# Values of two successive key tiles in one group of matmuls in the first attention, with a planner that prices changes of form on TensorE

## The chip, the cores and the metric

The kernel runs on one core of a Trainium2 chip. The metric is the device time of one execution in microseconds (us). Eight images pass through four layers in one launch. The core's engines are called PE (TensorE matmuls; PEld is its weight load), DVE (VectorE), ACT (ScalarE), POOL (GpSimd) and SP (SyncE, which here issues transfers).

## The reference, cut to what matters

An input `x` of 8 images with 256 channels and 32x32 pixels goes through four residual layers, each after a group norm. The first is an attention of 8 heads over the 1024 pixels, the second and third are 3x3 convolutions, the fourth is a mixer (four selective scans, gates, depthwise convolutions, a second attention, norms). The change touches the first layer:

```python
def _L0_conv_ref(x, w_qkv, w_out, b_out):
    HEADS, DIM_HEAD, SCALE, EPS = 8, 64, 10.0, 1e-12
    b, c, hh, ww = x.shape
    n = hh * ww
    qkv = jnp.einsum('bcxy,oc->boxy', x, w_qkv)
    q, k, v = jnp.split(qkv, 3, axis=1)
    q, k, v = (t.reshape(b, HEADS, DIM_HEAD, n) for t in (q, k, v))
    q, k = _l2norm_last(q), _l2norm_last(k)
    sim = jnp.einsum('bhdi,bhdj->bhij', q, k) * SCALE
    attn = jax.nn.softmax(sim, axis=-1)
    out = jnp.einsum('bhij,bhdj->bhid', attn, v)
    ...
    return jnp.einsum('bcxy,oc->boxy', out, w_out) + b_out[None, :, None, None]

x = x + _L0_conv_ref(_gn(x), ...)   # first attention
x = x + _L1_conv_ref(_gn(x), ...)   # 3x3 convolution
x = x + _L2_conv_ref(_gn(x), ...)   # 3x3 convolution
x = x + _L3_conv_ref(_gn(x), ...)   # mixer: scans, second attention, norms
return x
```

## The kernel before

**Streams and the planner.** The kernel's code does not issue its instructions in the order in which it is written. Every engine call is recorded (`Recorded`, line 252 makes the call later, so all planned work carries that line in the profile), with the stream it belongs to: A is the first attention (`front_attention`), O its output projection, C the two convolutions, N, F0 to F3, S and Z0 to Z3 the scans of the mixer, B and E its rest. Each stream exists once for each image. `Plan.issue` hands the records to `arrange`, which chooses one order for every engine. The streams of several images are mixed: while image 5 is in its first attention, image 4 is in its scans and image 3 in its second attention.

**How the order is made.** `gather` joins recorded matmuls into groups that are placed as a whole. `appraise` gives each group a length (`holds`). For matmuls it adds one length for each pass and a surcharge from the table `STAGGER`, by the form of the array: 64x128 means that the stationary operand has 64 rows and 128 columns. `rank` gives each group a due time, interpolated from the table `PACE`, which holds 4 marks for each stream and image. `arrange` plays the program forward with these lengths: on every engine it takes, of the groups that can start earliest, the one of the first rank (`pick`). When the next group on PE has another form than the last, 100 ns are added. The result is a fixed program order on each engine; on the chip each engine runs its own order and waits on semaphores.

**The first attention.** Heads go in pairs (`pair`): four pairs for an image, and for each pair two halves of 512 queries (`h`) and eight tiles of 128 keys (`kt`), so 64 units for an image. `scores` writes a unit's scores for both heads into one PSUM tile of 128x1024 (`big`, a pool of two buffers that almost all other matmuls share), by two matmuls of the form 64x128 that lie beside each other on different rows of the array; ACT then makes `p`, the exponential, in one instruction. `values` multiplies `p` with V into one PSUM tile `acc` (one buffer), by two matmuls of the form 128x64 that lie beside each other on different columns; eight units accumulate in one `acc`. DVE adds the `p` of an odd unit to that of the even one before it, and for every half four such sums go through `ones` (128x32 matmuls, `big<-p,ones`) to give the softmax's denominators. `p` tiles come from a pool of 12 buffers that most streams share. In the recorded order, `values` of a unit stands two units behind its `scores`: scores 2, values 0, scores 3, values 1, and so on.

In the profile one matmul of the program shows as two records, so a pair of scores is `big<-q,k` x4 and a pair of values is `acc<-p,v` x4. The second attention also writes `acc<-p,v` (and `cv<-p,v`); its code is not touched.

Of the kernel before, what the change touches and what calls it, by code (L numbers as in the profile page):

```python
# [25 lines left out]
NKT = N // P  # L26
# [5 lines left out]
ENGINES = {"PE": 0, "DVE": 1, "Activation": 2, "Pool": 3, "SP": 4}  # L32
TABLES = {"Exp": 1, "Abs": 1, "Tanh": 5, "Ln": 2, "Gelu": 4}
WINDOW = 3413.33
STAGGER = {(128, 128): 5, (64, 128): 109, (128, 64): 56, (128, 32): 29, (32, 128): 90}
CLAIMED = (("vp", "v"), ("xp", "x"))
OUT_OF_TURN = {("ps_big", "big")}
PACE = {
    "A": (
        (-682, -424, -117, -25),  # L40
        (516, 618, 694, 732),
        (1009, 1111, 1211, 1320),
        (1607, 1675, 1748, 1823),
        (2135, 2205, 2285, 2342),
        (2665, 2733, 2806, 2909),
        (3195, 3278, 3368, 3454),
        (3714, 3781, 3854, 3902),
    ),
    "B": (
        (1368, 1444, 1509, 1584),  # L50
        (1923, 1981, 2040, 2094),
        (2413, 2483, 2561, 2631),
        (2909, 2939, 3105, 3156),
        (3483, 3566, 3655, 3734),
        (4003, 4099, 4197, 4313),
        (4492, 4492, 4513, 4700),
        (5658, 5715, 5736, 5740),
    ),
    "C": (
        (268, 286, 475, 478),  # L60
        (226, 890, 1004, 1104),
        (1251, 1399, 1527, 1655),
        (1776, 1933, 2060, 2185),
        (2284, 2453, 2596, 2729),
        (2985, 3045, 3116, 3245),
        (3380, 3514, 3656, 3802),
        (3926, 4001, 4174, 4291),
    ),
    "E": (
        (1584, 1624, 1671, 1704),  # L70
        (2139, 2161, 2194, 2229),
        (2639, 2685, 2724, 2761),
        (3178, 3208, 3256, 3277),
        (3704, 3752, 3787, 3816),
        (3976, 3978, 4015, 4017),
        (4691, 4842, 5048, 5087),
        (4451, 4453, 4775, 4871),
    ),
    "F0": (
        (435, 494, 498, 499),  # L80
        (863, 968, 998, 1025),
        (499, 905, 905, 905),
        (608, 740, 740, 987),
        (1145, 1145, 1194, 1203),
        (1745, 1746, 1865, 1865),
        (3530, 3530, 3570, 3570),
        (2244, 2362, 2402, 2421),
    ),
    "F1": (
        (488, 661, 706, 713),  # L90
        (1324, 1375, 1376, 1386),
        (1814, 1825, 1853, 1909),
        (2387, 2404, 2435, 2467),
        (2826, 2842, 2888, 2939),
        (3472, 3479, 3485, 3495),
        (3877, 3894, 3932, 3935),
        (4379, 4441, 4506, 4578),
    ),
    "F2": (
        (760, 818, 839, 866),  # L100
        (1108, 1355, 1361, 1397),
        (1896, 1929, 1932, 2020),
        (2337, 2337, 2456, 2476),
        (2961, 2989, 2989, 3066),
        (3215, 3469, 3469, 3572),
        (3973, 4011, 4055, 4097),
        (4582, 4590, 4590, 4590),
    ),
    "F3": (
        (976, 979, 984, 1044),  # L110
        (1537, 1537, 1540, 1610),
        (2056, 2068, 2077, 2097),
        (2557, 2557, 2558, 2621),
        (3063, 3088, 3122, 3170),
        (3673, 3679, 3738, 3747),
        (4139, 4163, 4163, 4176),
        (4723, 4723, 4723, 4723),
    ),
    "N": (
        (-178, -178, -178, -178),  # L120
        (830, 830, 858, 860),
        (986, 986, 986, 998),
        (1734, 1734, 1734, 1734),
        (2043, 2043, 2043, 2043),
        (2294, 2297, 2315, 2323),
        (3328, 3374, 3374, 3374),
        (3310, 3532, 3543, 3563),
    ),
    "O": (
        (551, 553, 553, 558),  # L130
        (711, 711, 758, 828),
        (1298, 1319, 1360, 1374),
        (1850, 1851, 1863, 1863),
        (2373, 2401, 2418, 2418),
        (2891, 2915, 2915, 2915),
        (3458, 3480, 3482, 3486),
        (3923, 3923, 3928, 3928),
    ),
    "S": (
        (700, 900, 1070, 1202),  # L140
        (1245, 1449, 1589, 1768),
        (1761, 1972, 2117, 2288),
        (2279, 2491, 2632, 2808),
        (2832, 3034, 3177, 3349),
        (3344, 3565, 3701, 3868),
        (3878, 4092, 4264, 4402),
        (4841, 4852, 4853, 4853),
    ),
    "V": (
        (-584, -584, -364, -358),  # L150
    ),
    "Z0": (
        (796, 817, 859, 884),
        (1326, 1328, 1334, 1394),
        (1870, 1875, 1911, 1983),
        (2394, 2406, 2565, 2581),
        (2926, 2932, 2948, 2948),
        (3101, 3128, 3148, 3389),
        (3955, 3972, 3994, 4136),
        (4523, 4524, 4533, 4664),  # L160
    ),
    "Z1": (
        (687, 722, 730, 1159),
        (1431, 1453, 1457, 1554),
        (1971, 1990, 1992, 2018),
        (2454, 2496, 2509, 2607),
        (3049, 3055, 3071, 3091),
        (3562, 3574, 3585, 3627),
        (4091, 4091, 4099, 4159),
        (4701, 4701, 4701, 4719),  # L170
    ),
    "Z2": (
        (1011, 1011, 1011, 1011),
        (1595, 1595, 1659, 1674),
        (2072, 2072, 2075, 2076),
        (2615, 2622, 2635, 2656),
        (3215, 3216, 3218, 3222),
        (3561, 3561, 3561, 3568),
        (4204, 4250, 4250, 4250),
        (4758, 4759, 4759, 4759),  # L180
    ),
    "Z3": (
        (1299, 1312, 1326, 1326),
        (1709, 1734, 1745, 1865),
        (2260, 2284, 2383, 2388),
        (2794, 2795, 2812, 2836),
        (3329, 3334, 3339, 3339),
        (3847, 3848, 3855, 3867),
        (4301, 4301, 4341, 4393),
        (4764, 4836, 4836, 5061),  # L190
    ),
    "H": (
        (-2577, -2577, -2577, -2577),
        (-1990, -1988, -1950, -1759),
        (-2961, -2961, -2961, -2312),
        (-2311, -2311, -2311, -2311),
        (-1439, -1439, -1439, -1439),
        (-1171, -1171, -1171, -1168),
        (-608, -608, -608, -608),
        (-633, -633, -633, -411),  # L200
    ),
}

# [189 lines left out]
def gather(ops):  # L393
    groups, of = [], []
    for n, op in enumerate(ops):
        last = groups[-1] if groups else None
        if op["engine"] == 0:
            out, lhs = op["outs"][0], op["ins"][0]
            (rows, at), (width, to) = place(lhs), place(out)
            op["array"], op["at"] = (rows, width), (at, to)  # L400
            if last and (last.array, last.stream) == (op["array"], op["stream"]):
                first = ops[last.ops[0]]["outs"][0]
                if elements(out) <= P:
                    joins = len(last.ops) < 16
                elif op["array"] != (P, P):
                    joins = len(last.ops) < 4 and all(
                        ops[k]["at"] != op["at"] for k in last.ops
                    )
                else:
                    joins = len(last.ops) < 3  # L410
                beside = first.tensor.name == out.tensor.name or rows == 32
                if joins and beside:
                    last.ops.append(n)
                    of.append(len(groups) - 1)
                    continue
        groups.append(Group(op, n))
        groups[-1].array = op.get("array")
        of.append(len(groups) - 1)
    return groups, of
# [39 lines left out]
def appraise(ops, groups, rooms):  # L459
    for g in groups:  # L460
# [18 lines left out]
        for op in (ops[n] for n in g.ops):  # L479
            n = elements(op["outs"][0])  # L480
            if op["array"] != (P, P) and n > P and beside and op["at"] not in beside:
                beside.add(op["at"])
                continue
            beside = {op["at"]}
            g.holds += max(n / 0.6, 215 if g.holds else 135) + STAGGER[op["array"]]
        g.takes = g.holds + 165


# [33 lines left out]
def arrange(ops, rooms):  # L522
# [110 lines left out]
    def pick(e):  # L633
        chosen, at = None, 0
        candidates = ready[e]
        while at < len(candidates):
# [10 lines left out]
            late = start  # L647
            if groups[n].table and not groups[n].table & table:
                late += 1200.0
            if (  # L650
                chosen is None
                or late < chosen[0] - 1e-9
# [34 lines left out]
    while len(order) < len(groups):  # L687
# [8 lines left out]
        if e == 0:  # L696
            if g.array != array:
                if array:
                    holds, takes = holds + 100.0, takes + 100.0
                array = g.array  # L700
            now, rest = start, holds
            pass_windows(now)
# [46 lines left out]
def preact_stack(ctx: ExitStack, tc: tile.TileContext, I, out, cols):  # L749
# [460 lines left out]
    def attention(pairs):  # L1210
# [24 lines left out]
            scalar.activation(p, s, AF.Exp)  # L1235
            u["p"] = p

        def values(u):
            pair, h, kt = pair_of(u["t"]), u["h"], u["kt"]
            if kt == 0:  # L1240
                pair["acc"] = acc_tile()
            for e in range(2):
                tensor.matmul(
                    pair["acc"][e * 64 : e * 64 + 64],
                    pair["v"][e](kt),
                    u["p"][:, HALVES[e]],
                    start=kt == 0,
                    stop=kt == NKT - 1,
                )
            if kt == 0:  # L1250
                pair["sums"] = []
            if kt % 2 == 0:
                pair["sums"].append(u["p"])
            else:
                total = pair["sums"][-1]
                vector.tensor_add(total, total, u["p"])
            if kt == NKT - 1:
                pair["take"](h, pair["acc"], pair["sums"])

        units = [  # L1260
# [2 lines left out]
            for h in range(2)  # L1263
            for kt in range(NKT)
        ]
        for n in range(len(units) + 2):
            if n + 8 < len(units):
                pair_of(units[n + 8]["t"])
            for stage, at in ((scores, n), (values, n - 2)):
                if 0 <= at < len(units):  # L1270
                    stage(units[at])

    def front_attention(src, img, exact=False):
        img["src"] = src
# [1103 lines left out]
```

## Time and profile before

| | |
|---|---|
| median of 3 runs | 5156.42 us (5152.59 to 5157.5) |
| the profiled execution | 5152.86 us |
| its span, from first to last instruction | 5151.1 us |
| mean granted TensorE clock | 0.951 |
| matmuls of the program on PE | 9589 (19178 records) |

Engine lines give busy time, share of the span and number of instructions. A matmul's end in the profile is modelled, so successive matmuls overlap in the list by up to 0.2 us, and the distance from one start to the next is the safer number. In the list of engine groups the columns are operation, output and input tiles, form and shape, count, then busy us and mean ns of one, then the idle time before them with who ended it.

| group | count | busy us | mean ns | idle before us |
|---|---|---|---|---|
| PE `acc<-p,v` 128*64, both attentions | 3072 | 837.1 | 625 | 39.3 |
| PE `cv<-taps,w` 128*128 | 3072 | 748.9 | 395 | 33.9 |
| PE `big<-q,k` 64*128, first attention | 2048 | 584.0 | 650 | 31.1 |
| PE `y<-hs,sel` 128*32, scans | 2048 | 312.7 | 627 | 62.7 |
| PE `big<-qk,qk` 32*128, second attention | 2048 | 302.9 | 649 | 5.1 |
| ACT `p<-big` | 1024 | 1014.6 | 1020 | 567.7 |

The first attention's matmuls of the eight images start at 51, 268, 776, 1385, 1996, 2586, 3205 and 3781 us; the last of them starts at 4024 us. The last scan's `y<-hs,sel` stands at 4852 us.

### The profile page before, as it was taken

How to read it: one execution, taken by the hardware profiler on the slowest of the kernel's cores; microseconds unless marked ns; L12 is line 12 of the kernel's file. 1: busy time of each engine (PE TensorE's matmuls, PEld its weight loads, DVE VectorE, ACT ScalarE, POOL GpSimd, SP SyncE). 2: the span in 40 equal slices, each digit the busy share in tenths (PEclk: the TensorE clock that was granted, in tenths of full speed). 3: DMA queues.
4: the chain of work that ended last, by engine and by line, in shares of the span. 5: the costliest groups of instructions: out<-in, count | busy, mean ns of one | idle time of the engine just before them, and what ended most of it. 6: DMA issues, size and time to landing. Idle time of an engine off the chain costs nothing.

```text
span 5151.1 us, 53923 instructions
## 1 busy us (share of the span) xinstructions
PE 4757.1 (92%) x19178; PEld 1946.1 (38%) x19178; DVE 4037.5 (78%) x5586; ACT 2911.2 (57%) x3829; POOL 17.8 (0%) x26
## 2 busy tenths in 40 slices
PE   8999899999999999999999999999999899898796
PEld 3262263253432534344442344325343343432323
DVE  3336989987988968889886988878878899799802
ACT  4426446656665565656656555655656457476352
POOL 0000000000000000000000000000000000000000
PEclk9999899999999999999999999999999999898897
DMA  4143354343333433334423343324333444334200
GB/s 137 39 126 99 107 163 130 96 151 114 117 113 96 137 107 112 112 115 127 131 93 101 115 152 114 122 70 151 122 98 112 126 137 152 94 126 130 78 19 25
DMA packets 256662, 575.20 MB, mean 112 GB/s; under 512 B 51192, under 2 KB 79224, under 8 KB 256384
## 3 DMA queue, kind: packets, MB, share of 16 engines
q1 hardware_dynamic: 167680, 431.11, 26.7%
q10 hardware_dynamic: 88704, 140.55, 8.9%
q8 instruction: 154, 2.52, 0.2%
q14 instruction: 124, 1.02, 0.1%
HBM read 483.18 MB, written 63.18 MB: 106 GB/s over the span
## 4 chain that ended last, share of the span: by engine, by line
PE 66%; DVE 20%; ACT 6%; DMA 4%; issue 3%; SPq 1%; ACTq 0%; DVEq 0%
PE big L252 38%; PE cv L252 14%; PE acc L252 12%; DVE hs L252 11%; PE y L252 3%; ACT p L252 2%; DVE room L252 1%; DVE xt L252 1%; DVE p L252 1%; DVE u L252 1%; DMA rs<-inv 1%; SPq L252 1%; DVE st L252 1%; ACT taps L252 1%; DMA du<-du_m 1%
## 5 line engine op out<-in xcount | busy, mean ns | idle before, releaser
L252 ACT ACTIVATE p<-big 128x1024 f32<-128x1024 f32 x1024 | 1014.6, 1020 | 567.7 <-PE big L252 508.1
L252 ACT ACTIVATE da<-dt,a_neg 128x512 f32<-128x512 f32 x1024 | 728.0, 720 | 554.5 <-DVE hs L252 435.0
L252 PE MATMUL acc<-p,v 128*64 128x512 f32 x3072 | 837.1, 625 | 39.3 <-ACT p L252 36.1
L252 PE MATMUL cv<-taps,w 128*128 128x256 f32 x3072 | 748.9, 395 | 33.9 <-DVE taps L252 17.1
L252 PEld LDWEIGHTS cv<-taps,w 128*128 128x128 f32 x3072 | 583.8, 195 | 285.9 <-issue 152.8
L252 DVE TENSOR_TENSOR hs<-du,bc 128x1024 f32<-128x1024 f32 x512 | 613.4, 1209 | 78.6 <-PE y L252 56.5
L252 DVE TENSOR_TENSOR hs<-hs,bc 128x1024 f32<-128x1024 f32 x512 | 621.5, 1214 | 32.4 <-ACT carry L252 30.8
L252 DVE TENSOR_TENSOR_SCAN hs<-da,carry,hs 128x512 f32<-128x512 f32 x512 | 636.9, 1268 | 3.0 <-ACT da L252 2.3
L252 PE MATMUL big<-q,k 64*128 64x512 f32 x2048 | 584.0, 650 | 31.1 <-ACT p L252 20.7
L252 DVE TENSOR_TENSOR_SCAN hs<-da,hs 128x512 f32<-128x512 f32 x512 | 607.8, 1210 | 4.2 <-ACT da L252 2.9
L252 DVE TENSOR_TENSOR p<-p 128x1024 f32<-128x1024 f32 x256 | 311.6, 1217 | 207.0 <-ACT p L252 129.1
L252 PEld LDWEIGHTS acc<-p,v 128*64 128x64 f32 x3072 | 162.1, 136 | 599.6 <-issue 414.2
L252 PE MATMUL y<-hs,sel 128*32 128x512 f32 x2048 | 312.7, 627 | 62.7 <-DVE hs L252 52.0
L252 PEld LDWEIGHTS big<-q,k 64*128 64x128 f32 x2048 | 160.0, 188 | 424.9 <-issue 198.1
L252 PE MATMUL big<-qk,qk 32*128 32x512 f32 x2048 | 302.9, 649 | 5.1 <-DVE z L252 2.8
L252 PE MATMUL cv<-p,v 128*64 128x512 f32 x1024 | 278.7, 612 | 0.0
L252 PE MATMUL big<-xn,w 128*128 128x512 f32 x512 | 232.1, 599 | 2.3 <-ACT big L252 1.1
L252 PE MATMUL big<-o,w 128*128 128x512 f32 x384 | 179.4, 610 | 5.8 <-DVE o L252 4.0
L252 PE MATMUL big<-room,w 128*128 128x512 f32 (+3 forms) x308 | 145.0, 625 | 29.1 <-ACT room L252 28.5
L252 PEld LDWEIGHTS big<-qk,qk 32*128 32x128 f32 x2048 | 84.3, 185 | 188.5 <-issue 144.8
L252 PEld LDWEIGHTS y<-hs,sel 128*32 128x32 f32 x2048 | 47.4, 109 | 268.0 <-issue 116.5
L252 DVE RECIPROCAL few_inv<-few 128x16 f32<-128x16 f32 (+1 forms) x48 | 13.4, 279 | 168.7 <-DMA few<-sums 168.2
(235 smaller groups left out, 5190.8 us busy)
## 6 DMA issues: line engine op xcount, KB each, us to landing
bc<-bc SPq DMA_DIRECT2D x256, 512.0 KB
w<-wc ACTq DMA_DIRECT2D x384, 256.0 KB
dt<-dt_m SPq DMA_DIRECT2D x128, 512.0 KB
du<-du_m SPq DMA_DIRECT2D x128, 512.0 KB
rs<-inv SPq DMA_DIRECT2D x64, 256.0 KB
raw<-xm SPq DMA_DIRECT2D x64, 256.0 KB
dt_m<-dt SPq DMA_DIRECT2D x128, 128.0 KB
du_m<-a SPq DMA_DIRECT2D x128, 128.0 KB
```

The source lines that it names most:

```text
L252: made = op["call"](*args, **kwargs).ins
```

## The change

Three things are edited, and all marks of `PACE` but none of its streams are new.

First, `values` takes two units and issues their four matmuls one after the other, and the loop records two scores, then the values of the two units before them. `gather` lets such a group hold each place of the array twice where the form is 64 columns wide. Second, the lengths: every pass gets 5 ns instead of the surcharge of `STAGGER`, and a change of form gets the time of the new form from `SWITCH` instead of 100 ns. Third, `pick` can add `STAY` to a group that would change the form; `STAY` is 0.

```diff
-STAGGER = {(128, 128): 5, (64, 128): 109, (128, 64): 56, (128, 32): 29, (32, 128): 90}
+SWITCH = {(128, 128): 203, (64, 128): 203, (128, 64): 152, (128, 32): 125, (32, 128): 205}
+STAY = 0
...
 PACE = {
     "A": (
-        (-682, -424, -117, -25),
-        (516, 618, 694, 732),
+        (-1119, -855, -558, -455),
+        (331, 431, 506, 507),
...
@@ gather
-                    joins = len(last.ops) < 4 and all(
-                        ops[k]["at"] != op["at"] for k in last.ops
-                    )
+                    again = sum(ops[k]["at"] == op["at"] for k in last.ops)
+                    joins = len(last.ops) < 4 and again < (2 if width == 64 else 1)
@@ appraise
-            g.holds += max(n / 0.6, 215 if g.holds else 135) + STAGGER[op["array"]]
+            g.holds += max(n / 0.6, 215 if g.holds else 135) + 5
@@ arrange, pick
+            if e == 0 and groups[n].array != array:
+                late += STAY
@@ arrange
                 if array:
-                    holds, takes = holds + 100.0, takes + 100.0
+                    opens = SWITCH[g.array]
+                    holds, takes = holds + opens, takes + opens
@@ attention
-        def values(u):
-            pair, h, kt = pair_of(u["t"]), u["h"], u["kt"]
-            if kt == 0:
-                pair["acc"] = acc_tile()
-            for e in range(2):
-                tensor.matmul(
-                    pair["acc"][e * 64 : e * 64 + 64],
-                    pair["v"][e](kt),
-                    u["p"][:, HALVES[e]],
-                    start=kt == 0,
-                    stop=kt == NKT - 1,
-                )
-            if kt == 0:
-                pair["sums"] = []
-            if kt % 2 == 0:
-                pair["sums"].append(u["p"])
-            else:
-                total = pair["sums"][-1]
-                vector.tensor_add(total, total, u["p"])
-            if kt == NKT - 1:
+        def values(two):
+            pair, h = pair_of(two[0]["t"]), two[0]["h"]
+            if two[0]["kt"] == 0:
+                pair["acc"], pair["sums"] = acc_tile(), []
+            for u in two:
+                for e in range(2):
+                    tensor.matmul(
+                        pair["acc"][e * 64 : e * 64 + 64],
+                        pair["v"][e](u["kt"]),
+                        u["p"][:, HALVES[e]],
+                        start=u["kt"] == 0,
+                        stop=u["kt"] == NKT - 1,
+                    )
+            total = two[0]["p"]
+            vector.tensor_add(total, total, two[1]["p"])
+            pair["sums"].append(total)
+            if two[1]["kt"] == NKT - 1:
                 pair["take"](h, pair["acc"], pair["sums"])
...
-        for n in range(len(units) + 2):
+        for n in range(0, len(units) + 2, 2):
             if n + 8 < len(units):
                 pair_of(units[n + 8]["t"])
-            for stage, at in ((scores, n), (values, n - 2)):
-                if 0 <= at < len(units):
-                    stage(units[at])
+            for u in units[n : n + 2]:
+                scores(u)
+            if n:
+                values(units[n - 2 : n])
```

More of the change, by code (lines that the diff above doesn't have):

```diff
@@ L39 @@
     "A": (
-        (-682, -424, -117, -25),
-        (516, 618, 694, 732),
[L42 to L47, printed above, removed]
+        (-1119, -855, -558, -455),
+        (331, 431, 506, 507),
+        (813, 915, 1000, 1064),
+        (1478, 1523, 1564, 1564),
+        (1948, 2014, 2097, 2098),
+        (2474, 2542, 2615, 2660),
+        (2997, 3097, 3118, 3190),
@@ L48 @@
+        (3549, 3613, 3672, 3680),
     ),
     "B": (
[L50 to L57, printed above, removed]
+        (1198, 1212, 1244, 1268),
+        (1724, 1773, 1840, 1882),
+        (2238, 2297, 2383, 2456),
+        (2724, 2743, 2917, 2973),
+        (3293, 3372, 3469, 3551),
@@ L58 @@
+        (3722, 3869, 3989, 4125),
+        (4252, 4255, 4256, 4293),
+        (5965, 6024, 6103, 6134),
     ),
     "C": (
[L60 to L67, printed above, removed]
+        (102, 103, 107, 176),
+        (8, 727, 835, 931),
+        (1109, 1262, 1389, 1512),
+        (1565, 1748, 1880, 2001),
@@ L68 @@
+        (2108, 2265, 2413, 2543),
+        (2776, 2824, 2889, 2994),
+        (3092, 3318, 3467, 3609),
+        (3846, 3846, 4009, 4121),
     ),
     "E": (
[L70 to L77, printed above, removed]
+        (1379, 1426, 1482, 1526),
+        (1894, 2004, 2040, 2098),
@@ L78 @@
+        (2447, 2490, 2536, 2558),
+        (2942, 2955, 3033, 3062),
+        (3516, 3564, 3602, 3629),
+        (3084, 3127, 3153, 3169),
+        (4319, 4566, 4664, 4933),
+        (3410, 3723, 4016, 4016),
     ),
     "F0": (
[L80 to L87, printed above, removed]
+        (-528, -454, -454, -307),
@@ L88 @@
+        (94, 189, 191, 320),
+        (-38, 112, 136, 170),
+        (-1532, -914, -900, -654),
+        (1191, 1358, 1378, 1378),
+        (-221, -163, -140, -140),
+        (858, 858, 858, 858),
+        (-629, -585, -583, 154),
     ),
     "F1": (
[L90 to L97, printed above, removed]
+        (353, 479, 485, 485),
@@ L98 @@
+        (1137, 1198, 1198, 1198),
+        (1608, 1613, 1662, 1717),
+        (2174, 2242, 2254, 2286),
+        (2688, 2717, 2749, 2788),
+        (3264, 3264, 3280, 3282),
+        (3725, 3729, 3741, 3741),
+        (4213, 4213, 4303, 4303),
     ),
     "F2": (
[L100 to L106, printed above, removed]
@@ L107 @@
-        (4582, 4590, 4590, 4590),
+        (560, 695, 695, 813),
+        (519, 962, 1006, 1042),
+        (1757, 1777, 1777, 1811),
+        (1940, 1940, 2253, 2302),
+        (2737, 2803, 2815, 2933),
+        (2996, 3110, 3258, 3310),
+        (3772, 3838, 3889, 3921),
+        (4219, 4332, 4335, 4338),
     ),
     "F3": (
[L110 to L114, printed above, removed]
@@ L115 @@
-        (3673, 3679, 3738, 3747),
-        (4139, 4163, 4163, 4176),
-        (4723, 4723, 4723, 4723),
+        (842, 856, 856, 858),
+        (1272, 1290, 1470, 1470),
+        (1866, 1885, 1999, 1999),
+        (2385, 2391, 2467, 2520),
+        (2843, 2899, 2917, 2955),
+        (3511, 3517, 3595, 3605),
+        (3965, 4032, 4041, 4064),
+        (4382, 4437, 4447, 4447),
     ),
     "N": (
[L120 to L127, printed above, removed]
+        (-1228, -1054, -931, -931),
+        (-368, -105, -103, 105),
+        (-355, -355, -355, -355),
+        (446, 821, 836, 840),
+        (529, 687, 687, 1658),
+        (1233, 1236, 1770, 1810),
+        (3189, 3608, 3608, 3608),
+        (2401, 2763, 2870, 3562),
     ),
     "O": (
-        (551, 553, 553, 558),
-        (711, 711, 758, 828),
-        (1298, 1319, 1360, 1374),
@@ L133 @@
[L133 to L137, printed above, removed]
+        (368, 368, 368, 368),
+        (566, 575, 600, 662),
+        (1118, 1122, 1154, 1180),
+        (1620, 1674, 1674, 1686),
+        (2183, 2215, 2231, 2233),
+        (2672, 2702, 2702, 2727),
+        (3263, 3286, 3289, 3290),
+        (3690, 3741, 3743, 3756),
     ),
     "S": (
-        (700, 900, 1070, 1202),
@@ L141 @@
[L141 to L147, printed above, removed]
+        (611, 740, 906, 1038),
+        (1061, 1267, 1436, 1583),
+        (1571, 1788, 1915, 2101),
+        (2086, 2301, 2440, 2616),
+        (2684, 2786, 2960, 3119),
+        (3176, 3369, 3537, 3705),
+        (3712, 3946, 4107, 4251),
+        (4585, 4585, 4586, 4591),
@@ L148 @@
     ),
     "V": (
-        (-584, -584, -364, -358),
+        (-2785, -2717, -2717, -2690),
     ),
     "Z0": (
[L153 to L160, printed above, removed]
+        (623, 671, 803, 811),
+        (1160, 1165, 1189, 1209),
+        (1628, 1675, 1795, 2335),
+        (2111, 2112, 2216, 2576),
@@ L161 @@
+        (2772, 2786, 2787, 2813),
+        (2956, 2956, 3025, 3280),
+        (3815, 3849, 3849, 4264),
+        (4259, 4323, 4386, 4445),
     ),
     "Z1": (
[L163 to L170, printed above, removed]
+        (571, 574, 574, 884),
+        (1203, 1271, 1274, 1292),
@@ L171 @@
+        (1710, 1710, 1710, 1718),
+        (2277, 2305, 2315, 2322),
+        (2851, 2854, 2854, 2903),
+        (3421, 3422, 3422, 3489),
+        (3937, 3942, 4015, 4158),
+        (4373, 4373, 4397, 4397),
     ),
     "Z2": (
[L173 to L180, printed above, removed]
+        (766, 872, 872, 1035),
@@ L181 @@
+        (1443, 1478, 1484, 1484),
+        (1820, 1851, 1886, 1914),
+        (2414, 2416, 2418, 2418),
+        (2889, 2895, 2933, 3034),
+        (3296, 3349, 3392, 3396),
+        (4051, 4088, 4158, 4158),
+        (4406, 4532, 4586, 4678),
     ),
     "Z3": (
[L183 to L189, printed above, removed]
@@ L190 @@
-        (4764, 4836, 4836, 5061),
+        (1050, 1056, 1131, 1136),
+        (1538, 1542, 1590, 1653),
+        (2072, 2072, 2206, 2214),
+        (2604, 2606, 2636, 2676),
+        (3159, 3163, 3166, 3175),
+        (3671, 3672, 3688, 3688),
+        (4180, 4184, 4195, 4245),
+        (4447, 4457, 4458, 4556),
     ),
     "H": (
[L193 to L197, printed above, removed]
@@ L198 @@
-        (-1171, -1171, -1171, -1168),
-        (-608, -608, -608, -608),
-        (-633, -633, -633, -411),
+        (-4008, -3991, -3987, -3915),
+        (-3151, -3119, -3088, -1884),
+        (-4487, -4154, -3535, -1882),
+        (-4782, -4677, -4620, -1309),
+        (-2758, -2480, -2285, -949),
+        (-2380, -2380, -2262, -995),
+        (-2906, -2264, -1774, 141),
+        (-997, -844, -684, 319),
     ),
```

## The prediction

> **What bounds the kernel now.** I read the engines' shares first, then the chain of work that ended last, then PE's list in order of time, then who waits for whom, and last the busy time by stages.
>
> ```profile
> PE 4757.1 (92%) x19178; PEld 1946.1 (38%) x19178; DVE 4037.5 (78%) x5586; ACT 2911.2 (57%) x3829; POOL 17.8 (0%) x26
> ```
>
> ```profile
> PE 66%; DVE 20%; ACT 6%; DMA 4%; issue 3%; SPq 1%; ACTq 0%; DVEq 0%
> ```
>
> PE is busy for 92% of the span and holds 66% of the chain; DVE holds 20% of the chain. So time taken from PE shortens the run in most places, and not where a scan on DVE ends last. PE's idle time is 5151.1 - 4757.1 = 394 us.
>
> The list of PE in order of time (start, length, line, operation, tiles, form, count, idle before):
>
> ```profile
> 405.69 1.08 PE L252 MATMUL acc<-p,v 128*64 128x512 f32 x4
> 406.70 1.13 PE L252 MATMUL big<-q,k 64*128 64x512 f32 x4
> ...
> 409.74 2.79 PE L252 MATMUL acc<-p,v 128*64 128x512 f32 x12
> 412.47 1.99 PE L252 MATMUL big<-q,k 64*128 64x512 f32 x8
> 414.72 1.13 PE L252 MATMUL big<-q,k 64*128 64x512 f32 x4 [0.27 <-ACT p L252]
> ```
>
> ```profile
> 909.31 1.13 PE L252 MATMUL big<-q,k 64*128 64x512 f32 x4
> 910.37 1.08 PE L252 MATMUL acc<-p,v 128*64 128x512 f32 x4
> 911.37 1.07 PE L252 MATMUL y<-hs,sel 128*32 128x512 f32 x8
> 912.37 1.13 PE L252 MATMUL big<-q,k 64*128 64x512 f32 x4
> ```
>
> The reader is to see the price of a change of form, from start to next start. A pair of values between other forms takes 406.70 - 405.69 = 1.01 us. Three pairs in one run take 412.47 - 409.74 = 2.73 us. Two pairs more cost 1.72 us, so a pair inside a run costs 0.86 us, and opening the run costs 1.01 - 0.86 = 0.15 us. In the same way a pair of scores costs 910.37 - 909.31 = 1.06 us, so its form opens for 0.20 us; the four `y` (0.86 us of passes) take 1.00 us, so 128x32 opens for 0.14 us. The `big<-u,mdtw` x4 of form 128x128, from 903.25 to 905.17 us, takes 1.92 us against four passes of 0.43 us, which is 0.20 us for opening. The last line of the first block shows what stands against the change: a third score in a row waited for ACT to empty one of the two `big` buffers.
>
> ```profile
> PE big L252 <- ACT p L252: 51.1, 38, 8.0
> PE acc L252 <- ACT p L252: 36.1, 55, 6.8
> ```
>
> These are PE's waits for the exponential (us in total, times, longest): 87.2 us in 93 waits.
>
> ```profile
> 3000.00:3500.00 500.00, 474.93 (x1974) 199.03 (x1973) 410.29 (x595) 289.29 (x376) 1.80 (x1) 0.98 0.37 114
> 4700.00:4800.00 100.00, 70.43 (x260) 24.80 (x252) 98.44 (x104) 58.82 (x84) 1.80 (x1) 0.79 0.36 110
> ```
>
> The stages (window, length, busy us of PE, PEld, DVE, ACT, POOL, PE's granted clock, DMA share, GB/s) show PE as the bound while the first attentions run, up to 4024 us, and DVE as the bound in the last image's scan at 4700 us.
>
> **The change part by part.** *The work itself.* Both programs hold 9589 matmuls, and equal numbers of exponentials, DVE additions and DMAs (616 on ACT's queue, 1731 on SP's). One load of an activation table goes, 79 to 78, 1283 ns on ACT, which is 57% busy; I take it at nothing, and if ACT led there it would be 1.3 us.
>
> *Changes of form.* I count runs of one form in the two program orders. The counts before agree with the trace's for the two forms of this attention (817 and 508).
>
> - 128x64: 817 to 603, 214 fewer by 0.15 = 32.1 us.
> - 64x128: 508 to 341, 167 fewer by 0.20 = 33.4 us.
> - 128x128: 405 to 370, 35 fewer by 0.20 = 7.0 us.
> - 128x32: 314 to 329, 15 more by 0.14 = 2.1 us.
> - 32x128 (second attention): 257 in both.
>
> Sum: 70.4 us less on PE. It is spread over all images: by the stretches between their first scores 9, 9, 6, 10, 8, 8, 11 and 8 us.
>
> Whether a longer run hides its weight loads decides 0.15 us. The row is the run x12 above: three successive pairs on the same rows and columns, each at 0.86 us, with loads of 136 ns each (mean of `LDWEIGHTS acc<-p,v`) hidden. The Trainium skill speaks against it: "TensorE: Matmul & The Clock Gate", Part 3, "The mechanism", says that a weight load overlaps running matmuls only if it goes to other rows of the array. A merged pair of values would then pay its load, and 214 by an estimated 0.136 us, 29 us, would come back. The trace's row decides, so I take nothing for it.
>
> *The new wait.* A group of values now needs two exponentials instead of one, and scores come two in a row, each of which needs an emptied `big` buffer. Behind a waiting group stand, on PE's one queue, the scans' `y`, the convolutions' `cv` and the next scores, which all wait with it; behind them DVE waits for `y`. The exponential takes 1.02 us, and 0.1 us lies on each side of it in the list, so 1.2 us of other PE work are needed between a score and the next writer of its buffer, or the first user of its `p`. I laid the row prices along both orders and looked for places with less: 121 before, 203 after. What is missing there sums to 36.2 us before and 60.8 us after: 24.6 us more. From both sides: nothing, where a missing stretch falls into a wait that is there anyway (a values group and a score behind it can wait for the same exponential); and, as ACT also runs the scans' decays, 87.2 measured against 36.2 laid out is a factor of 2.4, so 59 us. I take 24.6 us, the value laid out.
>
> *The moved addition.* DVE's addition of two `p` stands behind four values instead of two. Its idle time is 5151 - 4037 = 1114 us, and the sums are first read by `big<-p,ones` at the end of a half. Nothing; if DVE led, a 1.22 us addition would be late once for each of 64 halves, 78 us, yet these additions stand inside 20% of the chain, so 16 us at most.
>
> *Every other stream is reordered by the new marks.* What I can compare: PE's work behind the last `y` of the last scan is 204 us before and 202 us after; DVE's work behind the last image's attention output falls by some 35 of 1040 us laid out. So no tail grows. For the idle time that the new order makes elsewhere there is no row; I take zero, and between -35 and +35 us, a tenth of the 394 us of idle either way.
>
> *How much reaches the end.* By windows the chain lies on PE for 84% (0 to 500 us), 45% (500 to 1000), 79% (1000 to 2000), 77% (2000 to 3000), 66% (3000 to 4000) and some 45% after. With each image's saving this is 49 of 70 us, a share of 0.69. The other end is PE's busy share, 0.92. I take 0.8.
>
> The sum: 0.8 x (-70.4 + 24.6) = -36.6 us. On the profiled execution, 5152.9 - 36.6 = 5116.3 us; that execution is 3.6 us below the median, so I expect a median of 5120. The bounds of the likeliest case: 0.92 x -70.4 = -65, 5092; and 0.69 x (-70.4 + 59) = -8, 5149.
>
> **The rivals.** *Slower: bunching.* Two scores in a row fill both `big` buffers, ACT is behind with decays, and PE stops at the third score, as at 414.72 us. It decides from where the 82 new places cost more than 70.4 / 82 = 0.86 us each. The waits of `big` for `p` average 51.1 / 38 = 1.34 us: 82 by 1.34 is 110 us, net +40 on PE, +32 at the end: 5188. For it: waits in the profile are 2.4 times what is laid out. Against it: the usual new order, two scores, four values, has 1.92 + 1.87 us of PE work for 2.04 us of ACT, and the waits of `acc` average only 0.66 us.
>
> *No change: DVE ends it anyway.* The scans set the pace from 480 us on, and PE arrives earlier only to wait for `hs`. Then only the first image's saving counts, about 9 us, 5147, or less. For it: 20% of the chain, 98% busy at 4700 us. Against it: from 600 to 4000 us DVE is idle for some 526 of 3400 us, enough to take up 70.
>
> *Much faster: the order has fewer waits as well.* Lengths that fit the chip let the planner meet its dates: all 70 us, and 10% of the idle time, 35 us: 5156 - 65 - 35 = 5056. For it: the old price of 100 ns for entering 128x128 is half of the row's 0.20 us. Against it: the old prices of the attention's forms (100 + 56, 100 + 109) already fit 0.15 and 0.20.
>
> *It doesn't do what it says:* then runs would not fall, but the program order shows them falling.
>
> **How the numbers follow.** The forecast, 5092 to 5149, has 0.50; much faster 0.18; no change 0.10; slower 0.22. A measurement of this kernel tells about 0.2%, 10 us, from no change. Faster, below 5146: most of the forecast and the much faster case, 0.69. Same: 0.09. Slower: 0.22. The range for 8 in 10 reaches from 5060 (nearly all of the much faster case's gain) to 5185 (nearly the bunching).
>
> **What would show it.** Right: PE's busy time falls by some 60 to 70 us, `acc<-p,v` from a mean of 625 ns towards 610 and `big<-q,k` from 650 towards 630, runs x8 of values at 1.87 us from start to start, and PE's waits for `p` grow from 87 to some 110 us. Wrong: waits for `p` over 170 us (bunching); PE's waits for `hs`, 52 us now, over 100 us (DVE); or x8 runs of values longer than 2 us (weight loads not hidden).

## The result, and the profile after

The change made the kernel slower: 5230.16 us, the median of 4 runs (5224.26 to 5237.1), against 5155.18 us before (4 runs). The ratio is 1.0151, with a 95% interval of 1.0139 to 1.0164. The profiled execution took 5224.26 us, its span is 5222.5 us, 71.4 us more than before.

The engines' shares and the chain that ended last, of the kernel after:

```profile
PE 4709.5 (90%) x19178; PEld 1981.0 (38%) x19178; DVE 4041.3 (77%) x5586; ACT 2897.9 (55%) x3828; POOL 17.8 (0%) x26
...
PE 62%; DVE 23%; ACT 7%; DMA 4%; issue 4%; SPq 1%; ACTq 0%; DVEq 0%
```

PE is busy for 47.6 us less, as the change meant. Its idle time is 5222.5 - 4709.5 = 513.0 us, against 394.0 before: 119.0 us more. The difference of the two is the whole loss, 71.4 us. DVE's and ACT's busy times moved by 4 and 13 us, so neither engine got more work; that they hold more of the chain fits PE's longer waits for them.

The list of PE in order of time, after (columns as before):

```profile
917.91 1.99 PE L253 MATMUL big<-q,k 64*128 64x512 f32 x8
919.83 1.94 PE L253 MATMUL acc<-p,v 128*64 128x512 f32 x8
921.70 3.70 PE L253 MATMUL big<-xn,w 128*128 128x512 f32 x8
...
3302.95 1.13 PE L253 MATMUL big<-q,k 64*128 64x512 f32 x4 [1.06 <-ACT p L253]
3305.20 1.13 PE L253 MATMUL big<-q,k 64*128 64x512 f32 x4 [1.12 <-ACT p L253]
3306.26 1.94 PE L253 MATMUL acc<-p,v 128*64 128x512 f32 x8
```

The first three lines are the new pattern as it was meant: two scores in 1.92 us, four values in 921.70 - 919.83 = 1.87 us, so 2 x 0.86 + 0.15, with the weight loads hidden. The last three show it where it fails: each score waits for the exponential of the score just before it, as if only one of the two `big` buffers were free, and no values stand between them to fill the 1.1 us.

PE's waits, after:

```profile
PE big L253 <- ACT p L253: 91.7, 65, 10.3
PE y L253 <- DVE hs L253: 53.5, 18, 7.2
PE acc L253 <- ACT p L253: 41.9, 57, 7.4
PE cv L253 <- DVE taps L253: 32.1, 19, 6.8
PE big L253 <- DVE local L253: 27.5, 7, 10.0
```

The last two of them, before:

```profile
PE cv L252 <- DVE taps L252: 17.1, 13, 6.1
PE big L252 <- DVE local L252: 16.0, 5, 5.9
```

Waits for the exponential `p` rose from 87.2 to 133.6 us. But that is 46.4 of the 119 us. The rest is spread: `taps` of the convolutions from 17.1 to 32.1 us, `local` of the mixer from 16.0 to 27.5, and many small ones. These streams' code was not touched; only their places were.

Among the waits for `p`, those of the first attention's scores grew most, from 20.7 to 76.7 us, while others fell (list of engine groups, before and after):

```profile
L252 PE MATMUL big<-q,k 64*128 64x512 f32 x2048 | 584.0, 650 | 31.1 <-ACT p L252 20.7
L253 PE MATMUL big<-q,k 64*128 64x512 f32 x2048 | 562.3, 651 | 90.5 <-ACT p L253 76.7
```

The first scan's first `y` came 13 us earlier than before (467 against 480 us), the last scan's last `y` 70 us later (4922 against 4852), and what follows it took 301 us against 299. With all `y` counted off in eighths, the ends of the eighths came 20, 12, 18, 38, 56, 60, 114 and 70 us later. So the loss grew over the middle of the run, unevenly, and neither start nor tail made it.

### The profile page after: what moved, and what is told of

The parts are those of the page before. It is cut to its first block, busy times and chain, and to the rows that moved or that the text cites. A ratio compares the mean times of both kernels' runs of the same rounds, so it can differ in the third digit from the quotient of the medians.

```text
span 5222.5 us, 53888 instructions
## 1 busy us (share of the span) xinstructions
PE 4709.5 (90%) x19178; PEld 1981.0 (38%) x19178; DVE 4041.3 (77%) x5586; ACT 2897.9 (55%) x3828; POOL 17.8 (0%) x26
## 4 chain that ended last, share of the span: by engine, by line
PE 62%; DVE 23%; ACT 7%; DMA 4%; issue 4%; SPq 1%; ACTq 0%; DVEq 0%
PE big L253 35%; PE cv L253 14%; DVE hs L253 12%; PE acc L253 11%; ACT p L253 3%; PE y L253 2%; DVE room L253 1%; DVE p L253 1%; DMA rs<-inv 1%; DVE xm L253 1%; DVE u L253 1%; SPq L253 1%; DVE st L253 1%; DVE xt L253 1%; ACT da L253 1%
## 5 line engine op out<-in xcount | busy, mean ns | idle before, releaser
L253 ACT ACTIVATE p<-big 128x1024 f32<-128x1024 f32 x1024 | 1003.4, 1019 | 487.5 <-PE big L253 417.3
L253 PE MATMUL acc<-p,v 128*64 128x512 f32 x3072 | 782.2, 618 | 47.3 <-ACT p L253 41.9
L253 PE MATMUL cv<-taps,w 128*128 128x256 f32 x3072 | 745.5, 395 | 41.1 <-DVE taps L253 32.1
L253 PE MATMUL big<-q,k 64*128 64x512 f32 x2048 | 562.3, 651 | 90.5 <-ACT p L253 76.7
L253 DVE TENSOR_TENSOR p<-p 128x1024 f32<-128x1024 f32 x256 | 311.9, 1218 | 142.8 <-PE acc L253 88.2
L253 PEld LDWEIGHTS acc<-p,v 128*64 128x64 f32 x3072 | 181.0, 138 | 587.7 <-issue 411.8
L253 PE MATMUL y<-hs,sel 128*32 128x512 f32 x2048 | 313.0, 630 | 57.3 <-DVE hs L253 53.5
L253 PEld LDWEIGHTS big<-q,k 64*128 64x128 f32 x2048 | 173.1, 192 | 448.6 <-ACT p L253 218.3
L253 DVE TENSOR_TENSOR xt<-xt,cv 128x512 f32<-128x512 f32 (+1 forms) x128 | 69.2, 550 | 138.3 <-PE cv L253 137.8
L253 PE MATMUL big<-raw,w 128*128 128x512 f32 x256 | 129.5, 648 | 22.8 <-DMA raw<-xm 9.4
```

The lines of the kernel that those rows point to most:

```text
L253: made = op["call"](*args, **kwargs).ins
```

## The experiments

Three theories were set against each other: "order" (the grouping is good, and the new order of everything else lost more), "bunching" (scores in twos and values in fours make PE wait for the exponentials), and "price" (a merged run does not save what it seemed to). The first two experiments put the grouping into the old order by hand and take it out of the new one, with all else left in its place.

### 1. The old order, values pulled together

```diff
+def put_together(ops, order):
+    quads, p_of, makes, last = quads_of(ops)     # values of an even and an odd key tile
+    for a0, a1, b0, b1 in quads:
+        at, made = order.index(a1), order.index(makes[p_of(b0)])
+        if order.index(b0) < at or made > at:
+            continue
+        if work_between(ops, order[order.index(last[p_of(b0)]) + 1 : at + 1]) < 1.0:
+            continue
+        for n in (b0, b1):
+            order.remove(n)
+        at = order.index(a1)
+        order[at + 1 : at + 1] = [b0, b1]
...
-        for n in arrange(self.ops, self.rooms):
+        for n in put_together(self.ops, arrange(self.ops, self.rooms)):
```

`work_between` adds up 0.43 us for each wide matmul and 0.2 us for each other one between the score of the odd key tile and the new place of its values.

> The order before, on every engine, with one thing moved: the values of the odd key tile are pulled forward to stand right behind those of the even one, wherever the exponential was made at least 1 us of PE work earlier. Runs of one form fall on PE from 2301 to 2048: 128x64 by 165, 64x128 by 83, 128x128 by 5. At the prices read from the trace before that is 165 x 0.15 + 83 x 0.20 + 5 x 0.20 = 42 us less. Theory 'order' (the grouping is good in itself, and what was lost was lost because all other work was put into a new and worse order): faster than before by 25 to 42 us, about 5120, and PE's waits for the exponential stay under 100 us. Theory 'bunching' (scores in twos and values in fours make PE wait for the exponentials): these waits grow by 40 us or more from 87, and the time is 5155 or more. Theory 'price' (a merged run does not save what the trace seemed to show, for instance because its weight loads are not hidden): PE's busy time falls by less than 20 us.

Measured: 5128.79 us, ratio 0.9955 (0.9939 to 0.9972); run again beside experiment 7, 0.9963 (0.9949 to 0.9977). Shares and waits of PE:

```profile
PE 4720.5 (92%) x19178; PEld 1972.6 (38%) x19178; DVE 4037.9 (79%) x5586; ACT 2904.4 (57%) x3829; POOL 17.8 (0%) x26
```

```profile
PE big L252 <- ACT p L252: 53.0, 42, 8.0
PE acc L252 <- ACT p L252: 38.2, 59, 6.8
```

PE's busy time fell by 36.6 of the 42 us laid out, so "price" falls. The waits for `p` are 91.2 us against 87.2, so "bunching" falls for this order. The span fell by 23.5 us, a little less than the 25 that "order" asked for at least; idle time rose by 13 us. This version is faster than both kernels.

### 2. The new order, pairs taken apart

```diff
+def take_apart(ops, order):
+    for k, (a0, a1, b0, b1) in enumerate(quads):
+        on_pe = [n for n in order[: order.index(a0)] if ops[n]["engine"] == 0][-4:]
+        if not all(ops[n]["array"] == (64, P) for n in on_pe):
+            continue
+        to = order.index(on_pe[2])               # ahead of the second pair of scores
...
+        for n in (a1, a0):
+            order.remove(n)
+            order.insert(to, n)
```

> The order after, on every engine, with one thing moved: where two pairs of scores stand right ahead of the four values, the first two values go between them, so that the order there is scores, values, scores, values, as it was before the change. Runs of one form rise from 1900 to 2194: 128x64 by 147, 64x128 by 147, at the prices of the trace 51 us more on PE. Theory 'order': slower than after by 40 to 51 us, about 5275. Theory 'bunching': the waits for the exponential fall from 134 us back to some 90, which pays for most of it, so 5230 or less, and if bunching were the whole loss, some 5160.

Measured: 5264.23 us, ratio 1.0219 (1.0202 to 1.0236) to the kernel before, so 34 us slower than after: a little under the 40 to 51 of "order", and well above the 5230 at most of "bunching".

```profile
PE 4759.7 (90%) x19178; PEld 1955.5 (37%) x19178; DVE 4042.9 (77%) x5586; ACT 2903.4 (55%) x3828; POOL 17.7 (0%) x26
```

```profile
PE big L253 <- ACT p L253: 79.8, 48, 9.9
PE acc L253 <- ACT p L253: 41.3, 57, 7.7
```

PE's busy time rose by 50.2 us where 51 were laid out. Waits for `p` fell from 133.6 to 121.1 us. So at the 147 places that the edit reaches, bunching exists and is worth 12.5 us, against 50 us of form changes that the pairs save. The other 109 of the 256 groups of four values, which have other work between them and the scores or a pair of scores alone, stayed as they were, so what bunching costs there was not measured.

The two experiments make a table of ratios to the kernel before (in neither are all groups moved; "together" has 2048 runs of one form in the old order and 1900 in the new, "apart" 2301 and 2194):

| | values apart | values together |
|---|---|---|
| old order | 1 | 0.9955 |
| new order | 1.0219 | 1.0151 |

Along the rows the grouping gains in both orders, 0.45% and 0.67%. Down the columns the new order loses 2.2% and 2.0%, over 100 us.

### 3 and 4. A new order without grouping

Third, the kernel before with every due time moved by 3 us; fourth, the kernel before with the new lengths alone:

```diff
+PACE = {
+    name: tuple(
+        tuple(m + 3 * (-1) ** (image + len(name)) for m in marks)
+        for image, marks in enumerate(rows)
+    )
+    for name, rows in PACE.items()
+}
```

> The kernel before with every due time moved by 3 us, one way for even images and the other way for odd ones (and by stream in turn); the recorded work, the groups and the prices are untouched, so the form changes stay (2288 runs against 2301). Theory 'order': the planner's order is so sensitive to its due times that this alone costs as much as the change did or more, 5200 to 5300, by PE's waits for many different producers. Theories 'bunching' and 'price': nothing in the attention's pattern has changed, so the time stays within 20 us of 5155.

> The kernel before with the new lengths alone (5 ns for each pass, and the time of the new form at a change), the old due times, and scores and values recorded one unit at a time as before. Runs of one form stay (2295). Theory 'order': any new order without due times fitted to it is worse, 5250 to 5330, with the waits of PE spread over many producers. Theory 'bunching': no pairs, so no loss: within 30 us of 5155, or faster, since the lengths fit the chip better.

Measured: 5321.0 us (ratio 1.0327, 1.0306 to 1.0348) and 5328.56 us (1.0342, 1.0321 to 1.0362). The first is worse than even "order" expected, the second at the upper end of its range. Of the kernel with due times 3 us off, the shares, PE's longest waits, and span and granted clock:

```profile
PE 4808.8 (90%) x19178; PEld 1966.1 (37%) x19178; DVE 4035.6 (76%) x5586; ACT 2906.8 (55%) x3829; POOL 17.8 (0%) x26
```

```profile
PE y L259 <- DVE hs L259: 71.2, 29, 6.5
PE big L259 <- ACT p L259: 64.5, 38, 7.0
PE acc L259 <- ACT p L259: 41.7, 64, 6.8
PE big L259 <- ACT room L259: 34.4, 8, 10.9
PE big L259 <- DVE local L259: 25.6, 8, 8.0
```

```profile
core 0: 5322.8 us, clock 0.938
```

The counts of instructions are the same on every engine, and yet PE idles for 120 us more and is also busy for 52 us more. Most of the second part is the clock. Its record holds only the values 1.0 and 0.5, so 0.938 instead of 0.951 means 660 us at half clock instead of 505 (two times the missing share, times the span). By that record PE was busy for 455 us of those, against 373 before. An estimate: if work takes twice as long there (the shortest `acc<-p,v` record before took 592 ns, the longest 1115), half of it is lost, 41 us more. Waits for `p` are 106 and 112 us in these two kernels, where the code pairs no scores: a new order alone can bring 19 to 25 of the 46 us by which they grew after the change.

### 5 and 6. Grouping with a replan

The fifth has the new `values`, loop and `gather`, with old lengths and old due times. The sixth plans the changed kernel's groups with its lengths, but ranks them by their places in the order before:

```diff
+        place = {n: k for k, n in enumerate(arrange(self.ops, self.rooms))}
+        again = in_twos(self.ops)
+        self.ops = [self.ops[n] for n in again]
+        places = [place[n] for n in again]
+        for n in arrange_as(self.ops, self.rooms, places):
-        for n in arrange(self.ops, self.rooms):
```

> The kernel before with the grouping alone (two scores, then the values of two units, and groups that hold each place twice), planned anew with the old lengths and the old due times. Runs of one form fall from 2301 to 1910, nearly as far as in the changed kernel (1900). Theory 'order': the saved form changes, some 68 us on PE, are swamped by the new order: 5250 to 5330, although the same grouping, put into the old order by hand, made the kernel 23 us faster. Rival, that the new lengths or the new due times carry the loss and not the replanning as such: 5090 to 5150.

> The changed kernel's grouping and lengths, but the due times are the places that the work had in the order before, so that the planner is asked to keep that order. The planner still takes what can start first and uses the due times only between candidates, so the order is not the same. Runs of one form: 1981. Theory 'order': somewhere between the order kept by hand (5129) and a replan with due times that do not fit (5320), about 5230, so that even the old order as a wish does not keep what the old order gave. Rival, that the fitted new due times are themselves what is wrong: 5090 to 5140.

Measured: 5341.28 us (1.0366, 1.0336 to 1.0396) and 5267.87 us (1.0223, 1.0193 to 1.0253), both some 10 to 40 us above what "order" expected, and far from its rivals. PE's longest waits in the fifth:

```profile
PE big L252 <- ACT p L252: 127.9, 77, 11.6
PE y L252 <- DVE hs L252: 65.9, 29, 6.9
PE acc L252 <- ACT p L252: 43.4, 55, 7.6
PE cv L252 <- DVE taps L252: 41.6, 18, 13.3
```

Grouping gains 23 us when the old order is kept, and the kernel loses 189 when the planner starts anew. Beside experiments 3 and 4, which were planned anew without it (5321 and 5329 us), grouping gains nothing here. With a poor order the waits for `p` can also grow, to 171 us here. Even the old places as a wish are not kept: the planner takes what can start first and asks for the rank only between equals, so one group of another length can shift all choices behind it.

### 7. More merging by hand

The first experiment's order, in which matmuls of the forms 128x64 and 128x32 of other streams (accumulating ones alone) are also pulled forward behind a run of their form:

```diff
-        for n in put_together(self.ops, arrange(self.ops, self.rooms)):
+        for n in same_forms(self.ops, put_together(self.ops, arrange(self.ops, self.rooms))):
```

> The order before with the values pulled together as in the first experiment, and then, in the same manner, other matmuls of the forms 128x64 and 128x32 pulled forward (by at most 4 us of planned time, and only if the planner had their inputs ready 0.5 us earlier) to stand behind a run of their form. Runs of one form fall from 2048 to 1964: 58 of 128x64, 13 of 128x32, 7 of 128x128, 5 of 64x128, 13 us by the trace's prices. Theory 'order' (form changes save their price where nothing else is reordered): 5 to 13 us below the first experiment, 5116 to 5124. Rival, that the order is full already and each pull costs some other wait as much: 5130 to 5160.

> The first experiment's kernel on the same chip as the one beside it, for the comparison. By it, a ratio of 0.9955 to the kernel before; all theories expect 0.994 to 0.997.

Measured: 5164.7 us, ratio 1.0026 (1.0016 to 1.0037), beside 0.9963 for the first experiment's kernel on the same chip. "Order" fails here, and the time is even 5 us above the rival's range: 84 fewer runs of one form, and yet a span of 5154.7 us against 5127.6. Its shares:

```profile
PE 4737.3 (92%) x19178; PEld 1992.2 (39%) x19178; DVE 4039.0 (78%) x5586; ACT 2900.0 (56%) x3829; POOL 17.7 (0%) x26
```

PE is busy for 17 us more than in experiment 1, of which 12 us are lost to half clock by the sum used in experiment 3 (195 against 183 us), and idle for 10 us more. The other 5 us stand where 13 us less were laid out. What each pull cost was not followed further.

## Why the prediction was wrong

**The price of a form change: right within a fifth where the prediction used it.** 0.15 and 0.20 us were read from a few rows. To compare, the change in time lost to half clock, estimated as in experiment 3, is taken off PE's busy time. The changed kernel lost 194.2 us to it against 186.5, so 47.6 + 7.7 = 55 us came off where 70.4 were laid out; experiment 1 (183.1 against 186.5) gives 36.6 - 3.4 = 33 of 42, experiment 2 (201.9 against 194.2) 50.2 - 7.7 = 42 of 51. That is four fifths three times, and where the last fifth goes was not traced. It is no rule: experiment 5, where PE was busy for 4764.9 us and lost 230.0, gives 36 of the 68 us expected, experiment 7 gives 5 us more instead of 13 less, and experiment 3 comes out 11 us higher though it has 13 runs fewer.

**Weight loads inside a run: right, by the row.** Four values on the same rows take 1.87 us from start to start with loads of 138 ns. The rule of the Trainium skill in "TensorE: Matmul & The Clock Gate", Part 3, "The mechanism", that a load overlaps only matmuls on other rows, does not show here; the same section also lets a load run ahead into a background weight buffer, which no run here can tell apart.

**The new wait: mis-sized, within its bounds.** 24.6 us were taken, between 0 and 59; the waits for `p` grew by 46.4. The second experiment gives 12.5 us of that to the 147 pairs that it takes apart, and the third and fourth show that replanning alone can bring 19 and 25 us. The scores' own waits for `p` are 77, 83 and 54 us in the three kernels that were planned with the grouping (after, experiments 5 and 6) against 39 and 40 in the two without it (experiments 3 and 4), so grouping may cost the planner more than the 12.5 us; that was not taken apart. The bunching rival named the right side, but the wait that it rests on is less than half of the 119 us.

**"Every other stream is reordered by the new marks ... I take zero, and between -35 and +35 us": this step failed.** The new order's idle time outside the waits for `p` grew by 119.0 - 46.4 = 73 us, and by the table of experiments 1 and 2 the new order as a whole costs over 100 us. I had compared the tails of the two orders, and these are indeed nearly equal (299 and 301 us), but a loss in the middle shows in no tail. The bound of a tenth of the idle time had no row behind it. The kernel before has one order that its due times happen to fit: moved by 3 us, they give one that is 170 us slower. Of the five orders that the planner made anew here, the changed kernel's included, all were slower than before, by 75 to 189 us, and the changed kernel's was the best. None of the prediction's three signs of being wrong appeared: the waits for `p` are 133.6 us, not over 170, those for `hs` 53.5, not over 100, and a run of four values takes 1.87 us, not over 2. It had named no sign for a worse order of the other streams.

**The share that reaches the end: roughly right.** 0.8 was taken between 0.69 and 0.92, of PE's saving less the new waits. In these terms experiment 1 gives 23.5 / (36.6 - 4.0) = 0.72, and experiment 2, whose span grew by 37.4 us, 37.4 / (50.2 - 12.4) = 0.99, a little above the bounds.

**DVE's moved addition: no cost seen.** DVE's idle time before `p<-p` fell, from 207.0 to 142.8 us.

**What stays open.** Which property makes one order of the planner better than another was not found; beside the scores' waits for `p`, the losses sit in many small waits of many streams. Nor did any run separate the new due times from the new lengths inside the changed kernel's own order.

## What to carry to other kernels

When an edit goes through a greedy scheduler, price two things apart: the edit at a fixed order, and the new order. The first can be read from a trace and was worth 0.45% here; the second is a draw that the trace of the old order did not bound, and against an order that fits it lost five times out of five. Keep the old order and move only the edited instructions, and a gain that would drown stays visible. That is no guarantee: more moves by hand, of other streams, lost 31 us in experiment 7.

## What the runs showed of the hardware

Opening a run of another form on TensorE costs 0.14 to 0.21 us in the five main forms of this kernel (four of them in the prediction's rows; the fifth, 32x128, by `big<-qk,qk` x8 at 2401.01 us before, 1.07 us to the next start less 0.86 of passes); for 128x64 it is the same 0.15 us in runs of two, four and six matmuls. What shows of it in PE's busy time when runs are merged or split is less: four fifths in three cases, half in experiment 5, nothing in experiment 7.

The clock falls not only after idle time. In the kernel before, PE ran 16 products of one column each, with no idle time listed before or within them (first fence: list of PE in order of time; second: window, length, busy us of PE, PEld, DVE, ACT, POOL, granted clock, DMA share, GB/s):

```profile
398.38 3.85 PE L252 MATMUL cv<-mean_w,ln_sq 128*128 128x1 f32 x32
```

```profile
395.00:400.00 5.00, 5.00 (x31) 2.60 (x27) 2.20 (x2) 4.56 (x5) 0.00 (x0) 1.00 0.00 0
400.00:402.00 2.00, 2.00 (x19) 2.00 (x19) 0.00 (x0) 0.00 (x0) 0.00 (x0) 0.96 0.00 0
402.00:405.00 3.00, 3.00 (x8) 0.94 (x9) 1.76 (x7) 0.00 (x0) 0.00 (x0) 0.50 0.00 0
```

Busy throughout, and in the next 3 us the granted clock is 0.50. It is not the only such place: in the kernel before, at each of the 23 stretches of at least 3.4 us of such products, the record of the clock falls to 0.5 within the stretch or less than 2 us behind it, and 16 of the 70 stretches at half clock begin after 3.4 us in which PE was busy for over 95%, most of it with such products. So a stretch of very narrow matmuls is followed by half clock here like a stretch of waiting. Most of the added half clock of experiment 3 is of the other kind: its stretches that begin after less busy work take 554 us, against 428 before, the others 102 against 75.
